# Truer durations and new places in a hand-planned two-layer Metaformer kernel, with small VectorE work moved to GpSimd

## The chip, the cores and the metric

One core of a Trainium2 chip runs the whole kernel. The metric is the device time of one execution in microseconds; the kernel before took 3854.12 us (median of three runs, 3846.69 to 3867.57). Engines are called as in the profile: PE (TensorE), DVE (VectorE), ACT (ScalarE), POOL (GpSimd) and SP (the queue that issues most transfers).

## What is computed

Two layers on an image batch `x` of (8, 256, 32, 32) in fp32, that is 8 images of 1024 tokens with 256 channels. Cut to what matters, the reference is:

```python
# layer 0
h = layernorm(x) @ W_in;  xs, z = split(h)            # 512 channels each
xs = silu(causal_conv4(xs));  dt, B, C = parts(xs @ W_x)
dt = softplus(dt @ W_dt + b_dt)
state = exp(dt * A) * state + dt * xs * B             # 16 states, over 1024 tokens
x += ((sum(state * C) + xs * Dp) * silu(z)) @ W_out
t = layernorm(x)                                      # mixture of 8 experts, best 2 per token
p = softmax(t @ gate_w + gate_b);  w = top2(p)
x += sum_e w[e] * (gelu(t @ W1[e] + b1[e]) @ W2[e] + b2[e])
# layer 1
y = layernorm(x)
x += concat(y[:128], conv3x3, conv1x11, conv11x1, mamba)   # each on 32 channels
t = layernorm(x);  r = t @ wr + br                    # of 1024 tokens the best 511
t += where(best, r * (gelu(t @ w1 + b1) @ w2 + b2), 0)
```

## The kernel before

**Tiling.** Layer 0's state-space part is cut into 16 units (8 images, two halves of 512 tokens). A unit has two channel pairs (`cp`), each of 8 steps over pairs of states, and each step handles two blocks of 128 channels by `scan_pair` (line 777): POOL multiplies dt*x with the broadcast B for two states (`dbu`, line 780, 128 x 1024), ACT makes the two exponentials (785), DVE runs two scans (788) and multiplies with C (793), and PE adds the results into the PSUM tile `y` by an identity matmul (804). In some steps POOL first adds the two products (797), which halves PE's part; the list `PAIRED` says in how many of a unit's steps. A unit has 64 scans, so 16 units have 1024; layer 1's small mamba has 32 scans for each group of two images. The scans come to 1152, and they serve below as a scale of progress. B and C rows are broadcast to all partitions by DMA (839, 1416).

**Stages.** After every unit, `tokens` projects to tokens and makes the layer norm and gate logits. After each four units (a group of 2 images, 2048 tokens) follow `route` (softmax, top 2, slots), `scatter` (the rows go to their slots by indirect DMA from POOL, `put`, 1068), `experts` (23 blocks of 256 rows: weights fetched by SP, two rounds of matmuls at 1157 and 1179, written back), `combine` (each token's two rows gathered by POOL at 1250, weighted and summed with the residual), `taps_of` (the depthwise convolutions, 26 sums on DVE, 1323), `mamba_in`, `mamba_scan`, `mamba_out`, `assemble`, `ranks` (each token's rank by counting on DVE, 1534 to 1545), `feed_forward` (best tokens to slots, two matmul layers) and `finish` (rows gathered at 1621 and added, output written).

**What sets the order.** The kernel doesn't issue its operations in the order of the text. Every stage records steps (`step`, `dma`, `gpsimd`): an engine, a duration in us, a due time, and the buffers read and written. `Flow.run` then plays the kernel through with these durations and takes, over and over, the step that can start first, with preference by due time; that gives each engine its fixed instruction order. On the chip every engine works its list strictly in order. Three kinds of numbers therefore shape the program: durations in the steps (`HOP` is the time from one engine's end to another's start, `PACE` a factor on PE's durations, `lat` the landing time of a transfer), the due times in `UNIT_AT` and `PLAN` (in units of two scans; a pair is the start and the distance of a stage's parts), and the sizes of the buffer pools (2 `ys`, 2 `wdiag`, 4 `dbu`, 4 `bc`). Where the planner sees PE idle, it puts matmuls on zeros there (`warm`, 525 and 529).

**The places concerned.** `delta` (line 747) computes softplus as max(v, 0) + ln(1 + exp(-|v|)): ACT makes |v| (754), the exponential (755) and the logarithm (756), DVE joins them into `dt` (758), and POOL multiplies dt with x (760). `small_rstd` (854) makes 1/sqrt(variance) on ACT and minus mean times that on DVE (859); `tokens` and `combine` use it. `gate` (910) turns raw logits into logits with four small DVE operations. In `combine` (1230) PE sums four products into PSUM for each block of 128 tokens:

```python
nc.tensor.matmul(at, g.ident, xc.v[:, h], start=True, stop=False)
for q in range(2):
    nc.tensor.matmul(at, ds.v[:, q], ys.v[:, q], start=False, stop=False)
nc.tensor.matmul(at, grp["cwt"].v[rows], b2[rows, blk % 4], start=False, stop=True)
```

where `ds` is a diagonal of the routing weights that ACT makes from the identity (1254), and ACT copies the sum out of PSUM (1267).

Of the kernel before, what the change touches and what calls it, by code (L numbers as in the profile page):

```python
# [38 lines left out]
N = 512  # L39
# [17 lines left out]
PAIRED = [2, 4, 0, 4, 3, 4, 7, 5, 5, 6, 8, 7, 5, 8, 6, 6, 7, 7, 5, 6]  # L57
# [5 lines left out]
    dict(put=10.59, experts=(180, 8.0), combine=(355, 4.88), taps=(436, 2.05), mamba=464, assemble=(486, 1.12), ranks=500, ffn=(521, 4.8), finish=(570, 2.4)),  # L63
    dict(put=6.24, experts=(357, 6.25), combine=(465, 1.5), taps=(550, 0.75), mamba=541, assemble=(568, 2.41), ranks=628, ffn=(722, 4.8), finish=(767, 3.75)),
    dict(put=5.3, experts=(465, 5), combine=(602, 2.94), taps=(701, 1.84), mamba=666, assemble=(681, 1.88), ranks=699, ffn=(791, 2.81), finish=(827, 2.89)),
    dict(put=2.65, experts=(603, 4), combine=(692, 0.86), taps=(761, 0.77), mamba=775, assemble=(796, 0.43), ranks=795, ffn=(836, 3), finish=(873, 3.07)),
# [30 lines left out]
HOP = 0.08  # L97
SWITCH = 1.3
PACE = 1.07
# [73 lines left out]
class Flow:  # L173
# [29 lines left out]
    def dma(self, prio, kb, run, reads=(), writes=(), fills=(), claims=(), us=0.4):  # L203
        return self.step(SP, us, prio, run, reads, writes, fills, claims, lat=2.3 + kb / 180)

    def run(self):
# [17 lines left out]
        def earliest(s):  # L224
            at = now[s.engine]
            for d in s.needs:
                at = max(at, d.end + (HOP if d.engine != s.engine or d.lat else 0.0))
# [71 lines left out]
def layers(g, ctx, x, a, out):  # L299
# [213 lines left out]
    def banks(n=1):  # L513
        return [buf("mm") for _ in range(n)]
# [232 lines left out]
    def delta(parts, dts, dtxs, xs, prio):  # L747

        v, l = banks(2), buf("sq")
        for n in range(2):  # L750
# [3 lines left out]
            step(ACT, 0.6, prio + 0.5, lambda n=n: nc.scalar.activation(l.v[:, n * N : (n + 1) * N], v[n].v, AF.Abs), [v[n]], fills=[l])  # L754
        step(ACT, 1.1, prio + 1, lambda: nc.scalar.activation(l.v, l.v, AF.Exp, scale=-1.0), [], [l], table="exp")
        step(ACT, 1.15, prio + 1, lambda: nc.scalar.activation(l.v, l.v, AF.Ln, bias=g.one), [], [l], table="exp")
        for n in range(2):
            step(DVE, 0.72, prio + 1.5, lambda n=n: nc.vector.scalar_tensor_tensor(
                dts.v[:, n], v[n].v, 0.0, l.v[:, n * N : (n + 1) * N], ALU.max, ALU.add), [v[n], l], fills=[dts])
        gpsimd(2.4, prio + 2, lambda: nc.gpsimd.tensor_tensor(dtxs.v, dts.v, xs.v, ALU.mult), [dts, xs], [dtxs])  # L760

    def dt_of(i, cp, prio):
# [6 lines left out]
        delta(parts, dts, dtxs, u[f"xs{cp}"], prio)  # L769
# [84 lines left out]
    def small_rstd(mv, rstd, shift, eps, prio, made, fill):  # L854
# [4 lines left out]
        return step(DVE, 0.6, prio, lambda: nc.vector.scalar_tensor_tensor(  # L859
            shift(), mv()[:, :, 0:1], -1.0, rstd(), ALU.mult, ALU.mult), [*made, fill[0]], fills=fill[1:])  # L860

    def tokens(i, prio):
# [47 lines left out]
        def gate():  # L910

            lg = grp["logits"].v[:, blks]
            wide = [P, nb, E]
            nc.vector.tensor_tensor(raw.v, raw.v, grp["rstd"].v[:, blks].to_broadcast(wide), ALU.mult)
            nc.vector.tensor_tensor(lg, gsum.to_broadcast(wide), grp["shift"].v[:, blks].to_broadcast(wide), ALU.mult)
            nc.vector.tensor_tensor(lg, lg, raw.v, ALU.add)
            nc.vector.tensor_tensor(lg, lg, gate_b.unsqueeze(1).to_broadcast(wide), ALU.add)

        step(DVE, 1.6, now, gate, [grp["rstd"], grp["shift"]], [raw], [grp["logits"]])

    def route(n, prio):
# [120 lines left out]
        for part in range(8):  # L1044
            step(DVE, 1.7, prio + 1 + 0.25 * part, lambda part=part: better(part), [lg], [r])
        step(DVE, 0.6, prio + 3, masks, [], [r])
        step(PE, 0.5, prio + 3, counts, [r], [pt])
        step(DVE, 1.0, prio + 3.5, sums, [pt], [r])
# [9 lines left out]
    def put(kind, dest, slots, index, src, grp, prio, name, sources):  # L1058
# [21 lines left out]
        step(POOL, 1.15, prio, run, sources, fills=[slots], lat=2.5)  # L1080
# [149 lines left out]
    def combine(n, prio, each):  # L1230
# [6 lines left out]
        for m in range(NI):  # L1237
# [600 lines left out]
```

## Time and profile before

| | us |
|---|---|
| median of the runs | 3854.12 |
| the profiled execution, its own time | 3870.05 |
| its span, first to last instruction | 3868.2 |
| scan 1025 starts | 2805.7 |
| scan 1088 ends | 2996.5 |
| no scan until | 3278.8 |
| scan 1120 ends | 3387.2 |
| no scan until | 3557.7 |
| last scan ends | 3653.1 |

The granted PE clock was 0.94 of full speed. DMA moved 676.67 MB, 175 GB/s on average. By the program's order, the first stretch without scans holds the rest of group 2's experts, group 1's assembling and ranking, and group 2's combining and taps; the second one the same stages one group later; what follows the last scan is group 3's assembling, ranking, feed-forward and finish. A group's row in the profile gives its line, engine, operation, tiles with shapes and count, then busy time and the mean of one in ns, then the idle time of the engine before it and what ended that.

```profile
DVE  4899899989679978976898898779787527557751
POOL 3567567588577768866775886545765433424522
DMA  6333333344544435535553558654669666967955
...
L780 POOL TENSOR_TENSOR dbu<-dtx,bc 128x1024 f32<-128x1024 f32 x576 | 1359.3, 2368 | 515.6 <-PE y L804 349.0
L788 DVE TENSOR_TENSOR_SCAN mm<-mm,dbu 128x512 f32<-128x512 f32 x576 | 703.9, 1222 | 229.7 <-ACT mm L785 153.8
L797 POOL TENSOR_TENSOR dbu<-dbu 128x512 f32<-128x512 f32 x370 | 480.9, 1301 | 299.4 <-DVE dbu L793 291.3
```

The digits are tenths of busy time in 40 slices of the span. VectorE is nearly full for the first three quarters and half empty in the last.

### The profile page before, as it was taken

The numbers are of one execution on the slowest core, as the hardware profiler recorded it, in microseconds if no ns is written. First come the engines' busy times: TensorE is split into PE (matmuls) and PEld (weight loads), VectorE is DVE, ScalarE is ACT, GpSimd is POOL, SyncE is SP. The second block draws the span as 40 slices with busy tenths as digits, with TensorE's granted clock in tenths as the row PEclk, the third lists the DMA queues.
The fourth block names the chain that finished last, engine by engine and source line by source line (L and its number), as shares of the span: only waits on it lengthen the run. The fifth ranks groups of instructions, "written<-read, shape, count | busy, mean of one in ns | idle before, by whom it ended". The sixth has DMA issues, their size and how long they took to land. (4 is left out here: it accounts for less than half of the span.)

```text
span 3868.2 us, 38209 instructions
## 1 busy us (share of the span) xinstructions
PE 3299.0 (85%) x10818; PEld 1849.4 (48%) x10818; DVE 2978.3 (77%) x4281; ACT 2207.2 (57%) x4010; POOL 2327.8 (60%) x1587
## 2 busy tenths in 40 slices
PE   8888888788889888978997798988987889799768
PEld 3333333333544444434553444554555666566446
DVE  4899899989679978976898898779787527557751
ACT  4555565465757557645765665665764456556433
POOL 3567567588577768866775886545765433424522
PEclk9999999999999999998999999999888989899989
DMA  6333333344544435535553558654669666967955
GB/s 232 122 123 131 114 131 132 106 151 162 200 139 167 165 129 194 181 111 172 172 174 122 195 181 226 204 184 136 200 204 223 222 213 214 243 215 215 247 175 168
DMA packets 277073, 676.67 MB, mean 175 GB/s; under 512 B 33063, under 2 KB 114349, under 8 KB 276862
## 3 DMA queue, kind: packets, MB, share of 16 engines
q1 hardware_dynamic: 258430, 623.88, 51.2%
q0 software_dynamic: 18432, 50.36, 4.1%
q8 instruction: 87, 1.43, 0.2%
q14 instruction: 124, 1.02, 0.1%
HBM read 572.92 MB, written 101.19 MB: 174 GB/s over the span
## 5 line engine op out<-in xcount | busy, mean ns | idle before, releaser
L780 POOL TENSOR_TENSOR dbu<-dtx,bc 128x1024 f32<-128x1024 f32 x576 | 1359.3, 2368 | 515.6 <-PE y L804 349.0
L804 PE MATMUL y<-dbu,ident 128*128 128x512 f32 x1564 | 822.6, 635 | 217.9 <-POOL dbu L797 185.7
L785 ACT ACTIVATE mm<-dt,neg_a 128x512 f32<-128x512 f32 x1152 | 770.3, 688 | 208.2 <-DVE dbu L793 190.4
L788 DVE TENSOR_TENSOR_SCAN mm<-mm,dbu 128x512 f32<-128x512 f32 x576 | 703.9, 1222 | 229.7 <-ACT mm L785 153.8
L793 DVE TENSOR_TENSOR dbu<-mm,bc 128x512 f32<-128x512 f32 x1152 | 796.4, 691 | 81.4 <-DMA bc<-rows 18.0
L788 DVE TENSOR_TENSOR_SCAN mm<-mm,state,dbu 128x512 f32<-128x512 f32 x576 | 738.2, 1282 | 59.5 <-POOL dbu L780 38.7
L797 POOL TENSOR_TENSOR dbu<-dbu 128x512 f32<-128x512 f32 x370 | 480.9, 1301 | 299.4 <-DVE dbu L793 291.3
L804 PEld LDWEIGHTS y<-dbu,ident 128*128 128x128 f32 x1564 | 281.6, 197 | 560.5 <-POOL dbu L797 278.7
L1179 PE MATMUL mm<-we,hid 128*128 128x256 f32 x1984 | 486.4, 398 | 36.0 <-ACT state L792 13.0
L792 ACT COPY state<-mm 128x1 f32<-128x1 f32 x576 | 91.4, 160 | 731.6 <-DVE dbu L793 710.9
L1157 PE MATMUL mm<-xbt,we 128*128 128x256 f32 x1984 | 474.3, 391 | 30.4 <-DMA we<-in_W12f 10.4
L1179 PEld LDWEIGHTS mm<-we,hid 128*128 128x128 f32 x1984 | 387.8, 199 | 156.3 <-issue 47.4
L1157 PEld LDWEIGHTS mm<-xbt,we 128*128 128x128 f32 x1984 | 383.4, 196 | 139.2 <-issue 46.9
L525 PE MATMUL y<-still 128*128 128x512 bf16 x1059 | 275.7, 395 | 0.0
L721 PE MATMUL mm<-pre,w_tap 128*128 128x512 f32 (+3 forms) x512 | 240.8, 612 | 28.6 <-ACT pre L708 27.3
L440 ACT ACT_TABLE_LOAD x176 | 225.8, 1283 | 3.1
L1250 POOL DMA_INDIRECT ys<-slots_y,slot x128 | 122.2, 954 | 160.0 <-PE mm L1262 69.0
L1163 ACT ACTIVATE hid<-mm,we 128x256 f32<-128x256 f32 x496 | 196.8, 475 | 37.8 <-PE mm L1157 29.1
L525 PEld LDWEIGHTS <-still 128*128 128x128 bf16 x1059 | 105.9, 101 | 192.6 <-issue 118.8
L721 PEld LDWEIGHTS mm<-pre,w_tap 128*128 128x128 f32 x512 | 95.5, 193 | 166.8 <-issue 103.9
L1068 POOL DMA_INDIRECT slots_x<-xg,slot x128 | 129.8, 1014 | 68.4 <-DVE acc_b L1323 31.2
L1621 POOL DMA_INDIRECT ys<-y,slot_t x64 | 63.1, 986 | 158.7 <-DVE xc L1631 59.0
(251 smaller groups left out, 3983.6 us busy)
## 6 DMA issues: line engine op xcount, KB each, us to landing
bc<-rows SPq DMA_DIRECT2D x512, 512.0 KB
bc<-rows SPq DMA_DIRECT2D x256, 256.0 KB
we<-in_W SPq DMA_DIRECT2D x92, 514.0 KB
we<-in_W SPq DMA_DIRECT2D x92, 512.0 KB
xb<-slots_x SPq DMA_DIRECT2D x92, 256.0 KB
slots_y<-xo SPq DMA_DIRECT2D x92, 256.0 KB
we<-in_W12f SPq DMA_DIRECT2D x32, 514.0 KB
xc<-x SPq DMA_DIRECT2D x64, 256.0 KB
```

What stands on the lines that cost most here:

```text
L440: nc.scalar.preload_act_table_set(tables[name])
L525: nc.tensor.matmul(live[0].v[:, 0], still, wide, start=False, stop=False)
L721: nc.tensor.matmul(tc_.v[:, cut:], w_tap[:, c, j], pre.v[:, cut + j : j + N], start=j == 3, stop=j == 0)
L780: gpsimd(2.45, prio, lambda: nc.gpsimd.tensor_tensor(dbu.v, dtxs.v[:, n : n + 1].to_broadcast(wide2), bt.v, ALU.mult), [dtxs, bt], [dbu], ...
L785: step(ACT, 0.69, prio, lambda j=j, h=h: nc.scalar.activation(h.v, dts.v[:, n], AF.Exp, scale=scales(j)), [dts], [h], table="exp", scan=True)
L788: step(DVE, 1.25, prio, lambda j=j, h=h: nc.vector.tensor_tensor_scan(h.v, h.v, dbu.v[:, j], 0.0 if initial is None else initial[1](j), AL ...
L793: step(DVE, 0.68, prio, lambda j=j, h=h: nc.vector.tensor_tensor(dbu.v[:, j], h.v, ct.v[:, j], ALU.mult), [h, ct], [dbu], scan=True)
L797: gpsimd(1.3, prio + 2.3, lambda: nc.gpsimd.tensor_tensor(dbu.v[:, 0], dbu.v[:, 0], dbu.v[:, 1], ALU.add), [], [dbu])
L804: nc.tensor.matmul(y.v[:, n], g.ident, dbu.v[:, j], start=False, stop=stop and (paired or j == 1))
L1157: nc.tensor.matmul(tv[:, f], we[0].v[:, at : at + P], xbt.v[:, k], start=k == 0, stop=k == KC - 1)
L1163: nc.scalar.activation(hid.v[:, f], tv[:, f % 2], func, bias=we[0].v[:, at : at + 1])
L1179: nc.tensor.matmul(to, hid.v[:, f, h * P : (h + 1) * P], we[1].v[:, f * C : (f + 1) * C], start=extra is None and f == 0, stop=f == FC - 1,)
```

## The change

It has four parts.

- **Durations and places.** The planner's durations of transfers (2.3 us + KB/180 becomes 3.4 us + KB/250), of indirect transfers and of several steps are set anew; a step that waits for PE now counts 0.15 us more (`DRAIN`); PE's factor goes from 1.07 to 1.05. `PLAN` and `PAIRED` get new values. None of this changes an operation, except that `PAIRED` decides where POOL adds pairs; it changes every engine's order.
- **dt.** Except in unit 0, ACT writes max(v, 0) into `dt` and POOL adds the logarithm, in place of DVE's two operations.
- **Small work.** The product in `small_rstd` becomes two POOL operations, and `gate` runs on POOL.
- **Late groups' rows.** In `combine` of groups 2 and 3 PE keeps the bias product only; DVE weights the two gathered rows onto it and adds the residual. The diagonals and ACT's copy fall away there.

The diff, with less context:

```diff
@@ -54,16 +54,16 @@
-PAIRED = [2, 4, 0, 4, 3, 4, 7, 5, 5, 6, 8, 7, 5, 8, 6, 6, 7, 7, 5, 6]
+PAIRED = [2, 2, 0, 4, 0, 5, 8, 5, 5, 7, 8, 8, 5, 5, 6, 5, 7, 7, 5, 5]
...
-    dict(put=10.59, experts=(180, 8.0), combine=(355, 4.88), taps=(436, 2.05), mamba=464, assemble=(486, 1.12), ranks=500, ffn=(521, 4.8), finish=(570, 2.4)),
-    dict(put=6.24, experts=(357, 6.25), combine=(465, 1.5), taps=(550, 0.75), mamba=541, assemble=(568, 2.41), ranks=628, ffn=(722, 4.8), finish=(767, 3.75)),
-    dict(put=5.3, experts=(465, 5), combine=(602, 2.94), taps=(701, 1.84), mamba=666, assemble=(681, 1.88), ranks=699, ffn=(791, 2.81), finish=(827, 2.89)),
-    dict(put=2.65, experts=(603, 4), combine=(692, 0.86), taps=(761, 0.77), mamba=775, assemble=(796, 0.43), ranks=795, ffn=(836, 3), finish=(873, 3.07)),
+    dict(put=2.64, experts=(180, 8.0), combine=(358, 2.93), taps=(451, 3.28), mamba=464, assemble=(496, 1.12), ranks=500, ffn=(521, 4.8), finish=(613, 2.21)),
+    dict(put=9.37, experts=(357, 6.25), combine=(505, 1.88), taps=(545, 1.2), mamba=551, assemble=(563, 2.41), ranks=630, ffn=(745, 3.84), finish=(768, 2.81)),
+    dict(put=5.28, experts=(465, 5), combine=(562, 2.94), taps=(659, 4.42), mamba=643, assemble=(684, 1.5), ranks=685, ffn=(791, 1.69), finish=(797, 4.62)),
+    dict(put=2.65, experts=(603, 4), combine=(692, 0.33), taps=(755, 1.54), mamba=775, assemble=(776, 0.43), ranks=753, ffn=(812, 3), finish=(841, 3.07)),
@@ -95,8 +95,9 @@
+DRAIN = 0.15
...
-PACE = 1.07
+PACE = 1.05
@@ -201,7 +202,7 @@
-        return self.step(SP, us, prio, run, reads, writes, fills, claims, lat=2.3 + kb / 180)
+        return self.step(SP, us, prio, run, reads, writes, fills, claims, lat=3.4 + kb / 250)
@@ -224,7 +225,7 @@
-                at = max(at, d.end + (HOP if d.engine != s.engine or d.lat else 0.0))
+                at = max(at, d.end + ((DRAIN if d.engine == PE else 0.0) + HOP if d.engine != s.engine or d.lat else 0.0))
@@ -744,7 +745,7 @@
-    def delta(parts, dts, dtxs, xs, prio):
+    def delta(parts, dts, dtxs, xs, prio, soon=False):
@@ -752,11 +753,17 @@
             step(ACT, 0.6, prio + 0.5, lambda n=n: nc.scalar.activation(l.v[:, n * N : (n + 1) * N], v[n].v, AF.Abs), [v[n]], fills=[l])
+            if not soon:
+                step(ACT, 0.6, prio + 0.6, lambda n=n: nc.scalar.activation(dts.v[:, n], v[n].v, AF.Relu), [v[n]], fills=[dts])
         step(ACT, 1.1, prio + 1, lambda: nc.scalar.activation(l.v, l.v, AF.Exp, scale=-1.0), [], [l], table="exp")
         step(ACT, 1.15, prio + 1, lambda: nc.scalar.activation(l.v, l.v, AF.Ln, bias=g.one), [], [l], table="exp")
-        for n in range(2):
-            step(DVE, 0.72, prio + 1.5, lambda n=n: nc.vector.scalar_tensor_tensor(
-                dts.v[:, n], v[n].v, 0.0, l.v[:, n * N : (n + 1) * N], ALU.max, ALU.add), [v[n], l], fills=[dts])
+        if soon:
+            for n in range(2):
+                step(DVE, 0.72, prio + 1.5, lambda n=n: nc.vector.scalar_tensor_tensor(
+                    dts.v[:, n], v[n].v, 0.0, l.v[:, n * N : (n + 1) * N], ALU.max, ALU.add), [v[n], l], fills=[dts])
+        else:
+            gpsimd(2.4, prio + 1.5, lambda: nc.gpsimd.tensor_tensor(
+                dts.v.rearrange("p n t -> p (n t)"), dts.v.rearrange("p n t -> p (n t)"), l.v, ALU.add), [l], [dts])
         gpsimd(2.4, prio + 2, lambda: nc.gpsimd.tensor_tensor(dtxs.v, dts.v, xs.v, ALU.mult), [dts, xs], [dtxs])
@@ -766,7 +773,7 @@
         ]
-        delta(parts, dts, dtxs, u[f"xs{cp}"], prio)
+        delta(parts, dts, dtxs, u[f"xs{cp}"], prio, soon=i == 0)
@@ -856,8 +863,12 @@
             nc.scalar.activation(rstd(), rstd(), AF.Exp, scale=-0.5)), made, fills=fill[:1], table="exp")
-        return step(DVE, 0.6, prio, lambda: nc.vector.scalar_tensor_tensor(
-            shift(), mv()[:, :, 0:1], -1.0, rstd(), ALU.mult, ALU.mult), [*made, fill[0]], fills=fill[1:])
+
+        def product():
+            nc.gpsimd.tensor_tensor(shift(), mv()[:, :, 0:1], rstd(), ALU.mult)
+            nc.gpsimd.tensor_scalar(shift(), shift(), -1.0, None, ALU.mult)
+
+        gpsimd(0.3, prio, product, [*made, fill[0]], fills=fill[1:])
@@ -911,12 +922,12 @@
-            nc.vector.tensor_tensor(raw.v, raw.v, grp["rstd"].v[:, blks].to_broadcast(wide), ALU.mult)
-            nc.vector.tensor_tensor(lg, lg, gate_b.unsqueeze(1).to_broadcast(wide), ALU.add)
-
...
+            nc.gpsimd.tensor_tensor(raw.v, raw.v, grp["rstd"].v[:, blks].to_broadcast(wide), ALU.mult)
...
+        gpsimd(0.8, now, gate, [grp["rstd"], grp["shift"]], [raw], [grp["logits"]])
@@ -1042,10 +1053,10 @@
-            step(DVE, 1.7, prio + 1 + 0.25 * part, lambda part=part: better(part), [lg], [r])
+            step(DVE, 1.9, prio + 1 + 0.25 * part, lambda part=part: better(part), [lg], [r])
...
-        step(DVE, 1.0, prio + 3.5, sums, [pt], [r])
+        step(DVE, 1.7, prio + 3.5, sums, [pt], [r])
@@ -1077,7 +1088,7 @@
-        step(POOL, 1.15, prio, run, sources, fills=[slots], lat=2.5)
+        step(POOL, 1.4, prio, run, sources, fills=[slots], lat=3.0)
@@ -1242,30 +1253,50 @@
             (t,), xo = banks(), buf("xo")
+
+            late = n >= 2
             for h in range(2):
                 blk = i * NI + j + h
-                ys, ds = buf("ys", line), buf("wdiag", line)
+                ys, ds = buf("ys", line), None if late else buf("wdiag", line)
                 for q in range(2):
...
                         in_offset=bass.IndirectOffsetOnAxis(ap=idx.v[:, blk : blk + 1], axis=0)),
-                        [grp["y"], idx], fills=[ys], lat=2.5)
-                    step(ACT, 0.4, now - 1, lambda q=q, ds=ds, wt=wt, blk=blk: nc.scalar.activation(
-                        ds.v[:, q], g.ident, AF.Copy, scale=wt.v[:, blk]), [wt], fills=[ds])
+                        [grp["y"], idx], fills=[ys], lat=3.3)
+                    if not late:
+                        step(ACT, 0.4, now - 1, lambda q=q, ds=ds, wt=wt, blk=blk: nc.scalar.activation(
+                            ds.v[:, q], g.ident, AF.Copy, scale=wt.v[:, blk]), [wt], fills=[ds])
...
                     at = t.v[:, h * C : (h + 1) * C]
-                    nc.tensor.matmul(at, g.ident, xc.v[:, h], start=True, stop=False)
-                    for q in range(2):
-                        nc.tensor.matmul(at, ds.v[:, q], ys.v[:, q], start=False, stop=False)
-                    nc.tensor.matmul(at, grp["cwt"].v[rows], b2[rows, blk % 4], start=False, stop=True)
-
-                step(PE, 1.9, now, product, [ys, ds, xc, grp["cwt"]], [t], claims=[xo])
+                    if ds is not None:
+                        nc.tensor.matmul(at, g.ident, xc.v[:, h], start=True, stop=False)
+                        for q in range(2):
+                            nc.tensor.matmul(at, ds.v[:, q], ys.v[:, q], start=False, stop=False)
+                    nc.tensor.matmul(at, grp["cwt"].v[rows], b2[rows, blk % 4], start=ds is None, stop=True)
+
+                def weighted(h=h, blk=blk, ys=ys, xo=xo, t=t):
+                    nc.vector.scalar_tensor_tensor(
+                        xo.v[:, h], ys.v[:, 0], grp["weight0"].v[:, blk], t.v[:, h * C : (h + 1) * C], ALU.mult, ALU.add
+                    )
+                    nc.vector.scalar_tensor_tensor(
+                        xo.v[:, h], ys.v[:, 1], grp["weight1"].v[:, blk], xo.v[:, h], ALU.mult, ALU.add
+                    )
+
+                if late:
+                    step(PE, 0.5, now, product, [grp["cwt"], xc], fills=[t], claims=[xo])
+                    step(DVE, 1.2, now + 0.2, weighted, [ys, t, grp["weight0"], grp["weight1"]], fills=[xo])
+                else:
+                    step(PE, 2.3, now, product, [ys, ds, xc, grp["cwt"]], [t], claims=[xo])
             bn = buf("bn")
-            step(ACT, 0.6, now + 0.3, lambda xo=xo, t=t: nc.scalar.copy(
-                xo.v, t.v.rearrange("p (h c) -> p h c", h=2)), [t], [xo])
+            if late:
+                step(DVE, 0.9, now + 0.3, lambda xo=xo, xc=xc: nc.vector.tensor_tensor(
+                    xo.v, xo.v, xc.v, ALU.add), [xc], [xo])
+            else:
+                step(ACT, 0.6, now + 0.3, lambda xo=xo, t=t: nc.scalar.copy(
+                    xo.v, t.v.rearrange("p (h c) -> p h c", h=2)), [t], [xo])
             dma(now + 0.5, 256, lambda xo=xo, two=two, i=i: nc.sync.dma_start(x1.v[:, two, i], xo.v), [xo], fills=[x1])
@@ -1418,7 +1449,7 @@
-                    dma(pos + 2 * sp + hf - 6, 512, fetch, [grp["rows"][hf]], [both[j]], us=0.8)
+                    dma(pos + 2 * sp + hf - 6, 800, fetch, [grp["rows"][hf]], [both[j]], us=0.9)
@@ -1486,7 +1517,7 @@
-            step(DVE, 1.9, now + 0.7, stats, [xc], [bn, junk], [tok])
+            step(DVE, 1.0, now + 0.7, stats, [xc], [bn, junk], [tok])
@@ -1621,7 +1652,7 @@
-                    [grp["y2"][i], slot], fills=[ys], lat=2.5)
+                    [grp["y2"][i], slot], fills=[ys], lat=3.3)
@@ -1638,7 +1669,7 @@
-            step(DVE, 1.3, now, added, [tok, ys], [xc])
+            step(DVE, 1.6, now, added, [tok, ys], [xc])
```

More of the change, by code (lines that the diff above doesn't have):

```diff
@@ L913, in gate @@
             wide = [P, nb, E]
-            nc.vector.tensor_tensor(raw.v, raw.v, grp["rstd"].v[:, blks].to_broadcast(wide), ALU.mult)
-            nc.vector.tensor_tensor(lg, gsum.to_broadcast(wide), grp["shift"].v[:, blks].to_broadcast(wide), ALU.mult)
-            nc.vector.tensor_tensor(lg, lg, raw.v, ALU.add)
-            nc.vector.tensor_tensor(lg, lg, gate_b.unsqueeze(1).to_broadcast(wide), ALU.add)
-        step(DVE, 1.6, now, gate, [grp["rstd"], grp["shift"]], [raw], [grp["logits"]])
+            nc.gpsimd.tensor_tensor(raw.v, raw.v, grp["rstd"].v[:, blks].to_broadcast(wide), ALU.mult)
+            nc.gpsimd.tensor_tensor(lg, gsum.to_broadcast(wide), grp["shift"].v[:, blks].to_broadcast(wide), ALU.mult)
+            nc.gpsimd.tensor_tensor(lg, lg, raw.v, ALU.add)
+            nc.gpsimd.tensor_tensor(lg, lg, gate_b.unsqueeze(1).to_broadcast(wide), ALU.add)
+        gpsimd(0.8, now, gate, [grp["rstd"], grp["shift"]], [raw], [grp["logits"]])
     def route(n, prio):
```

## The prediction

> **What bounds the kernel now.** I read the page's shares and its forty slices first, then the engines' busy time by stretch, cut where the timeline shows VectorE's scans stop or start (line 788, 1152 in all), then the groups by shape, then the waits, all and those of the first gap.
>
> ```profile
> span 3868.2 us, 38209 instructions
> PE 3299.0 (85%) x10818; PEld 1849.4 (48%) x10818; DVE 2978.3 (77%) x4281; ACT 2207.2 (57%) x4010; POOL 2327.8 (60%) x1587
> 58.00:1000.00 942.00, 807.35 (x2210) 352.09 (x2209) 860.50 (x1058) 512.56 (x910) 637.52 (x365) 0.96 0.39 133
> 1000.00:2000.00 1000.00, 865.01 (x2690) 467.82 (x2689) 818.96 (x993) 625.01 (x1104) 700.99 (x442) 0.95 0.48 162
> 2000.00:2996.50 996.50, 847.92 (x2788) 494.34 (x2787) 830.42 (x1137) 612.50 (x1102) 647.99 (x415) 0.93 0.62 187
> 2996.50:3278.80 282.30, 249.93 (x1070) 184.85 (x1070) 144.29 (x383) 147.34 (x301) 106.12 (x136) 0.94 0.67 214
> 3278.80:3387.20 108.40, 82.11 (x297) 57.04 (x296) 60.10 (x63) 60.12 (x106) 48.51 (x28) 0.87 1.01 244
> 3387.20:3557.70 170.50, 161.03 (x666) 111.96 (x665) 99.22 (x288) 96.08 (x204) 63.69 (x62) 0.96 0.67 211
> 3557.70:3653.10 95.40, 67.80 (x252) 39.40 (x251) 80.41 (x77) 54.58 (x98) 61.91 (x41) 0.93 0.96 254
> 3653.10:3868.20 215.10, 166.59 (x734) 119.45 (x732) 73.84 (x253) 75.15 (x156) 49.05 (x60) 0.89 0.56 178
> ```
>
> A row is: stretch, length, busy PE, weight loads, DVE, ACT, POOL, clock, DMA share, GB/s. Up to 2996.5 (the body, 1088 scans) DVE is busiest of the engines that do real work: 91%, then 82% and 83%. PE's 85% of the span holds 340 us of matmuls on zeros that keep its clock up (lines 525, 529). Then come two gaps without scans (282 and 170 us, PE 89% and 94%), two scan stretches whose DMA share is 1.01 and 0.96, and a tail of 215 us.
>
> ```profile
> L859 DVE SCALAR_TENSOR_TENSOR rs<-mv,rs 128x2 f32<-128x2 f32 x32 | 39.3, 1229 | 21.3 <-ACT rs L858 14.4 <-ACT rs L857 4.9 <-issue 1.2
> L859 DVE SCALAR_TENSOR_TENSOR shift<-mv,rstd 128x4 f32<-128x4 f32 x16 | 28.3, 1768 | 3.0 <-ACT rstd L858 3.0
> L758 DVE SCALAR_TENSOR_TENSOR dt<-mm,sq 128x512 f32<-128x512 f32 x72 | 46.4, 683 | 64.2 <-ACT sq L756 57.4 <-ACT state L792 6.8
> ...
> L859 DVE SCALAR_TENSOR_TENSOR rs<-mv,rs x32: 151/164/8916, 1775.7 to 3499.7; 128x2 f32<-128x2 f32 x32
> ...
> L760 POOL TENSOR_TENSOR dtx<-dt,xs 128x1024 f32<-128x1024 f32 x36 | 85.7, 2380 | 120.9 <-DVE dt L758 109.7 <-ACT xg L1579 9.3 <-ACT mm L785 1.8
> ...
> DVE mm L788 <- ACT mm L785: 174.6, 101, 9.4
> ...
> POOL slots_x L1068 <- DVE acc_b L1323: 31.2, 1, 31.2
> ```
>
> Two elements per partition take 0.16 us at the median and 8.9 at worst: DVE is held, not working. POOL stood 109.7 us for DVE's dt. The last row is gap A: POOL stood 31.2 us behind DVE, which still had group 3's routing and group 1's taps.
>
> **What the skill says.** The Trainium skill, "SBUF — State Buffer", section "Who interferes with whom": a DVE instruction with two SBUF inputs shares an exclusive port with a POOL instruction that reads SBUF, and the later one waits in full. The trace agrees: line 859 (both inputs in SBUF) has 0.164 at the median and 8.916 at most, while line 758, which reads PSUM, stays at 0.683. "GPSIMD Engine Reference", section 8, calls VectorE about twice as fast for elementwise work; here POOL's 128x512 add takes 1.301 and DVE's 0.691.
>
> **The change, part by part** (mean durations; counts from the two built programs).
>
> 1. DVE loses small_rstd's product (16 x 1.768 + 32 x 1.229 = 67.6), the gate (16 x (0.725 + 0.446 + 0.322 + 0.179) = 26.8) and dt's add but for unit 0 (68 x 0.683 = 46.4): 140.8 us, 118.4 of it in the body.
> 2. POOL gains dt's add (34 x 2.38 = 80.9), the gate (64 operations at an estimated 0.30, from 2.368 for 1024 elements and 1.301 for 512: 2.08 ns each and 0.23 fixed: 19.2) and the product as two operations (96 x 0.19, by its 3-element copy at 0.187: 18.2). PAIRED drops 22 pair additions (28.6). Net +89.7, some +84 before scan 1024, on an engine busy 65 to 70% there. Behind the add stand dt's product and the next dbu; four dbu buffers cover about two scans' pairs. In exchange the 109.7 us for DVE's dt becomes a wait for ACT alone. Cost bounds: minus 60 (half of that wait comes back as earlier dbu) to plus 84 (all on the path). I take 0 and let it reduce part 4's share.
> 3. ACT gains 68 relus (0.598: +40.7), loses 64 diagonals (0.395) and 16 copies (0.588): +6. PE loses 96 matmuls of 256 columns, two records each. Records at 0.216 (16 records in 3.45 us in the chain), so 0.432: −41, in the gaps. DVE gains 64 weightings (0.580 as line 1631) and 16 adds (0.691): +48 in the gaps; PE's wait for a gathered row becomes a wait of in-order DVE, behind which ranking stands.
> 4. Body before scan 1024 (0 to 2806): DVE −122 (part 1, and 4 taps later). The body is 14% idle and POOL gets fuller, so I take 65%: **−80**. All of it would be −122, and if POOL eats it, 0 or more.
> 5. Scans 1024 to 1088 (193 us): work comes in. Group 3's routing and scattering, 14 taps of group 1 and 70 expert matmuls (4.4 blocks of 16) make DVE 152 to 197, PE 125 to 171 (without zeros). I take **+35** (bounds 15 and 45).
> 6. Gap A (282.3): expert matmuls 332 to 198 (−58), combine's 64 to 16 (−21), transposes −6: PE −85; DVE −49 (21 taps and routing gone). It consists of 116 us until combine's first gather at 3112.3, 88 of combine, 79 to the next scan. The first loses half its expert blocks and the 31.2 us stall: 60. Combine still gathers through two ys buffers, 5 us a row block: 85. The rest has taps behind mamba's input instead of ahead: 65. Sum 210, **−72** (bounds −95, and −15 if gathers rather than matmuls set it).
> 7. The scan stretches at a DMA share of about 1 move the same bytes: **0**. A fetch planned as 800 KB is issued earlier, but the queues are full.
> 8. Gap B (170.5): expert matmuls 166 to 264 (+42), combine −21, transposes and zeros +11: PE +32; **+25** (bounds 10 and 40).
> 9. Tail: expert matmuls 230 to 196 (−15), three taps more (+5), but the chain (assemble, ranks, slots, feed-forward, gathers) has the same length: **−5** (bounds −20 and +10).
>
> SP's queue holds the same transfers in another order: group 3's scatter loads no longer stand in gap A ahead of experts' weights; I count that in part 6 only.
>
> Sum −80 + 35 − 72 + 25 − 5 = −97. The profiled execution took 3870.05 (span 3868.2, 1.9 around it), 16 above the median of the runs, 3854.12. Against the median: 3757.
>
> **Rivals.**
>
> (a) Slower: POOL takes DVE's place. Mechanism: dt's add and product hold POOL 4.75 us in a row, and each of 32 such pairs in the body lets the dbu buffers run dry. It decides once POOL is over some 85% busy where the scans run; at 800 to 1000 us it is 168 of 200 already. Price: part 4 turns from −80 into about +50 (76 for 32 adds, less a third of part 1): sum +33, **3887**. For: POOL waits 349 us for PE to free dbu, so the ring is tight. Against: those waits are slack that the additions can fill.
>
> (b) The gaps don't shrink: gathers, 5 us per block through two buffers, and DVE standing for them set gap A; part 6 is −15, sum −40, **3814**. For: POOL's 35.8 us wait for combine's matmul in gap A. Against: 85 us less on an engine at 89%.
>
> (c) More: truer durations also remove stalls of the order itself. DVE waited 174.6 us for ACT's exponentials; half gone is −87, less overlap with part 4: sum about −170, **3684**. For: many waits of 5 to 10 us where an engine's next instruction came late. Against: the reordering can make as many.
>
> That nothing changes in the order is excluded: the listing differs from the first rows on, and by whole stages in the gaps.
>
> **Numbers.** Forecast 0.45, (a) 0.20, (b) 0.17, (c) 0.18. Anything within 0.5% (about 19 us, what a measurement of this kernel can tell) counts as no change. Faster: 0.45 + 0.18 + 0.10 of (b) = 0.73. Same: 0.07 of (b) and 0.02 of (a): 0.09. Slower: 0.18. The forecast's own bounds are 3715 to 3800; the range runs from 3670, past (c), to 3885, just short of (a)'s centre, which leaves out about a tenth above and less below.
>
> **What would show it.** Right: the 1025th scan begins near 2725 instead of 2806, gap A near 210, gap B near 195, both scan stretches unchanged, POOL's wait for dt gone from VectorE. (a) shows as scans waiting for dbu more than the 110.9 us of now; (b) as gap A above 260; (c) as DVE above 90% through the body. Wrong in kind: if the scans' mean spacing before 2806 grows while DVE's work there falls.

## The result, and the profile after

The kernel after took 3825.99 us (median of 7 runs, 3818.1 to 3831.99), the kernel before beside it 3858.48 (7 runs): ratio 0.9909, 95% interval 0.9885 to 0.9934. It is faster by 0.9%; 2.5% was forecast. First the shares and two rows of slices of the kernel after, then the stretches cut at the same scans as before (stretch, length, busy PE, weight loads, DVE, ACT, POOL, clock, DMA share, GB/s).

```profile
span 3816.4 us, 38121 instructions
PE 3294.9 (86%) x10769; PEld 1846.5 (48%) x10769; DVE 2911.4 (76%) x4181; ACT 2208.1 (58%) x3999; POOL 2421.6 (63%) x1772
...
DVE  4889789879678887875899888668788757566651
...
POOL 3667478487667758987885887655774644426522
```

```profile
2787.90:3021.60 233.70, 203.67 (x737) 132.69 (x736) 196.92 (x242) 139.21 (x230) 137.93 (x101) 0.91 0.76 213
3021.60:3204.90 183.30, 160.66 (x682) 113.76 (x682) 122.43 (x326) 104.01 (x196) 83.54 (x104) 0.93 0.75 235
3204.90:3313.30 108.40, 79.55 (x289) 54.76 (x288) 65.95 (x68) 63.80 (x115) 59.50 (x39) 0.92 0.97 258
3313.30:3507.60 194.30, 184.52 (x788) 134.79 (x787) 122.18 (x325) 111.01 (x215) 75.71 (x92) 0.93 0.75 239
3507.60:3604.20 96.60, 80.06 (x279) 50.28 (x277) 71.07 (x77) 51.81 (x97) 57.31 (x35) 0.86 0.98 256
3604.20:3816.40 212.20, 154.78 (x667) 108.09 (x667) 74.30 (x252) 68.63 (x141) 50.32 (x63) 0.85 0.52 164
```

| stretch, us | before | after | change | forecast |
|---|---|---|---|---|
| to scan 1025 (the body) | 2805.7 | 2787.9 | −18 | −80 |
| scans 1025 to 1088 | 190.8 | 233.7 | +43 | +35 |
| gap A | 282.3 | 183.3 | −99 | −72 |
| scans 1089 to 1120 | 108.4 | 108.4 | 0 | 0 |
| gap B | 170.5 | 194.3 | +24 | +25 |
| scans 1121 to 1152 | 95.4 | 96.6 | +1 | 0 |
| tail | 215.1 | 212.2 | −3 | −5 |

The late stretches moved the way that was forecast, gap A a little past its bound of −95. The body didn't: the forecast's largest term brought less than a quarter. The table is of one profiled execution of each kernel. Its changes sum to −52, where the medians differ by 32, since the execution before took 3870.05 (median 3858.48) and the one after 3818.10 (median 3825.99); so some 20 us of the table belong to these two executions. The next four fences are the same two views for both kernels: first the whole body as one stretch, before and after, then what VectorE waited for in it (us in total, times, longest).

```profile
0.00:2805.70 2805.70, 2417.84 (x7277) 1235.28 (x7277) 2369.74 (x3053) 1669.78 (x2967) 1881.97 (x1194) 0.95 0.49 161
```

```profile
0.00:2787.90 2787.90, 2431.68 (x7333) 1252.08 (x7334) 2258.54 (x2895) 1669.64 (x3007) 1957.23 (x1342) 0.95 0.50 161
```

```profile
DVE mm L788 <- ACT mm L785: 164.5, 97, 9.4
DVE dt L758 <- ACT sq L756: 50.0, 7, 32.9
DVE mm L788 <- POOL dbu L780: 34.7, 15, 11.4
DVE raw L899 <- ACT xo L891: 23.1, 17, 4.0
```

```profile
DVE mm L795 <- ACT mm L792: 191.3, 114, 10.9
DVE mm L795 <- POOL dbu L787: 85.6, 37, 14.5
DVE dt L762 <- ACT sq L759: 35.9, 2, 32.9
DVE raw L910 <- ACT xo L902: 34.2, 20, 5.4
```

VectorE did lose its work: 2369.7 to 2258.5, 111 us of the 122 forecast. But its idle time in the body rose from 436.0 to 529.4, by 93. Scans (line 795 of the kernel after) wait more for their inputs, the exponentials from ACT and `dbu` from POOL. GpSimd's rows show what it took over: its waits in the body, before and then after, and three of its groups after.

```profile
POOL dtx L760 <- DVE dt L758: 103.3, 18, 14.8
```

```profile
POOL dt L765 <- ACT state L799: 28.0, 5, 11.8
POOL dt L765 <- ACT sq L759: 20.2, 7, 5.8
POOL dtx L767 <- DVE dt L762: 11.8, 1, 11.8
```

```profile
L765 POOL TENSOR_TENSOR dt<-dt,sq 128x1024 f32<-128x1024 f32 x34 | 81.9, 2409 | 92.5 <-ACT sq L759 64.5 <-ACT state L799 28.0
L869 POOL TENSOR_SCALAR rs<-rs 128x2 f32<-128x2 f32 x32 | 7.8, 242 | 2.8
L868 POOL TENSOR_TENSOR rs<-mv,rs 128x2 f32<-128x2 f32 x32 | 6.6, 208 | 19.8 <-ACT rs L865 15.6 <-DVE dbu L800 2.4 <-issue 0.8
```

The wait for VectorE's dt is gone but for unit 0 (48 us of waiting for ACT, in front of the new addition, stand in its place), and the two-element product that held VectorE 1.229 us at the mean costs GpSimd 0.45.

### The profile page after: what moved, and what is told of

Read it like the earlier page. It is cut to its first block, busy times and chain, and to the rows that moved or that the text cites. A ratio compares the mean times of both kernels' runs of the same rounds, so it can differ in the third digit from the quotient of the medians.

```text
span 3816.4 us, 38121 instructions
## 1 busy us (share of the span) xinstructions
PE 3294.9 (86%) x10769; PEld 1846.5 (48%) x10769; DVE 2911.4 (76%) x4181; ACT 2208.1 (58%) x3999; POOL 2421.6 (63%) x1772
## 5 line engine op out<-in xcount | busy, mean ns | idle before, releaser
L811 PE MATMUL y<-dbu,ident 128*128 128x512 f32 x1608 | 846.5, 636 | 214.3 <-POOL dbu L804 163.4
L804 POOL TENSOR_TENSOR dbu<-dbu 128x512 f32<-128x512 f32 x348 | 450.2, 1294 | 253.0 <-DVE dbu L800 244.4
L811 PEld LDWEIGHTS y<-dbu,ident 128*128 128x128 f32 x1608 | 292.1, 198 | 570.3 <-POOL dbu L804 256.9
L1190 PE MATMUL mm<-we,hid 128*128 128x256 f32 x1984 | 497.4, 404 | 34.0 <-ACT hid L1174 26.1
L526 PE MATMUL y<-still 128*128 128x512 bf16 x1130 | 294.8, 396 | 0.0
L1079 POOL DMA_INDIRECT slots_x<-xg,slot x128 | 128.9, 1007 | 46.4 <-ACT xg L1118 24.5
```

What stands on the lines that cost most here:

```text
L526: nc.tensor.matmul(live[0].v[:, 0], still, wide, start=False, stop=False)
L804: gpsimd(1.3, prio + 2.3, lambda: nc.gpsimd.tensor_tensor(dbu.v[:, 0], dbu.v[:, 0], dbu.v[:, 1], ALU.add), [], [dbu])
L811: nc.tensor.matmul(y.v[:, n], g.ident, dbu.v[:, j], start=False, stop=stop and (paired or j == 1))
L1190: nc.tensor.matmul(to, hid.v[:, f, h * P : (h + 1) * P], we[1].v[:, f * C : (f + 1) * C], start=extra is None and f == 0, stop=f == FC - 1,)
```

## The experiments

Theory: a microsecond taken from VectorE is worth much less than the 0.65 that part 4 counted. Rivals: GpSimd, whose added 84 us were priced at nothing, gave the gain back; the new order (durations, `DRAIN`, places, `PAIRED`) costs in the body; TensorE, at 86%, is the bound. All ratios are to the kernel before. "Order kept" means that the planner's durations stay and only the size of an operation on the chip changes, so that every engine has the same instruction list.

**What an engine's time is worth, in the same order.** Each of six kernels leaves something out. In the first pair that is dt's join in all but one column: VectorE's two operations in the kernel before, GpSimd's addition in the kernel after.

```diff
-                dts.v[:, n], v[n].v, 0.0, l.v[:, n * N : (n + 1) * N], ALU.max, ALU.add)
+                dts.v[:, n, :1], v[n].v[:, :1], 0.0, l.v[:, n * N : n * N + 1], ALU.max, ALU.add)
```

> The kernel before, every engine's order kept, but VectorE's two operations that join max(v, 0) and the logarithm into dt are cut from 512 columns to 1 (ScalarE's logarithm goes straight into dt); left out: max(v, 0) in dt, so the scans run on other values. It takes some 42 us off VectorE and gives nothing to GpSimd. Theory 1 (the body's pace is set by waits through short buffer rings and in-order engines; VectorE time that is freed becomes VectorE idle): 0 to 12 us faster than before. Theory 2 (VectorE's time was worth its full value and the work added on GpSimd ate it in the changed kernel): 30 to 45 us faster than before.

> The changed kernel, every engine's order kept, but GpSimd's addition that makes dt is cut from 1024 columns to 1 (the logarithm goes straight into dt); left out: max(v, 0) in dt. It takes some 77 us off GpSimd (34 of 2.38). Theory 1 (rings and order): at most 20 us faster than the changed kernel, so a ratio to before of 0.986 to 0.992. Theory 2 (GpSimd pays back what VectorE won): 40 to 75 us faster than the changed kernel, a ratio of 0.971 to 0.981.

Measured: 3827.51 against 3845.6, ratio 0.9949 (0.9926 to 0.9972): 20 us come back of the 38 that the two operations' busy time fell by (46.4 to 8.1), between the ranges of the two theories. Without GpSimd's addition the kernel after took 3803.7, ratio 0.9888 (0.9867 to 0.9909), only some 8 us less than with it, of 73 (81.9 to 9.0), and the two intervals overlap. GpSimd's addition isn't what ate the gain.

Larger cuts, one engine at a time: the product with C on 384 of 512 columns (VectorE), the sums of y on 384 columns (TensorE, before and after), the pair additions on 320 columns (GpSimd).

```diff
-                dbu.v[:, j], h.v, ct.v[:, j], ALU.mult), [h, ct], [dbu], scan=True)
+                dbu.v[:, j, :384], h.v[:, :384], ct.v[:, j, :384], ALU.mult), [h, ct], [dbu], scan=True)
```

> The kernel before, order kept; VectorE's multiplication with C (line 793) covers 384 of 512 columns, which leaves a quarter of the products out of the result and takes about 156 us off VectorE (128 columns at some 1.06 ns, 1152 times; 139 us of it before scan 1024). Theory 1 (rings and order set the pace, no single engine): 40 to 80 us faster, since b_dt_empty gave 20 for 42. Theory 5 (TensorE's release of dbu buffers sets it): less than 45 us. Theory of the prediction (65% and more of VectorE's time comes back): 95 us and more.

> The kernel before, order kept; TensorE's additions of the scans' products into y (line 804) cover 384 of 512 columns but for each y's last step, which leaves part of the sum out and takes about 148 us off TensorE (684 matmuls of two passes, 0.108 us each pass; some 130 us before scan 1024). Theory 5 (TensorE's release sets the pace; before's runs are about 3 us faster for each 0.001 more of granted clock): 80 to 148 us faster. Theory 1: 30 to 70 us. Theory of the prediction (VectorE bounds the body, TensorE only the gaps): less than 25 us.

> The kernel before, order kept; GpSimd's additions of pairs (line 797) cover 320 of 512 columns, which leaves part of the sum out and takes about 148 us off GpSimd (0.40 us, 370 times). GpSimd's addition stands between VectorE's product and TensorE's sum. Theory 1: 10 to 50 us faster. Theory 5: 10 to 40. If GpSimd sets the pace (rival (a)): 80 us and more. a_dt_empty, where 77 us less on GpSimd gave about 8, speaks for the low end.

> The changed kernel, order kept, with the same cut of TensorE's additions into y: about 152 us less on TensorE. Theory 5: VectorE has been relieved, so TensorE is worth at least as much as in b_pe_cut: a ratio to before of 0.955 to 0.972 where the changed kernel has 0.991. Theory 1: 0.973 to 0.983.

| cut | us removed | ratio, 95% interval | us gained |
|---|---|---|---|
| VectorE, before | 155 | 0.9775 (0.9729 to 0.9822) | 87 |
| GpSimd, before | 151 | 0.9915 (0.9890 to 0.9941) | 33 |
| TensorE, before | 138 | 1.0019 (1.0000 to 1.0039) | none |
| TensorE, after | the same cut | 0.9921 (0.9882 to 0.9961) | none beside 0.9909 |

The us removed are differences of the groups' busy times. The body as one stretch, for the cuts of VectorE, TensorE and GpSimd in the kernel before:

```profile
0.00:2719.70 2719.70, 2403.11 (x7277) 1237.43 (x7277) 2246.26 (x3053) 1667.54 (x2967) 1874.88 (x1194) 0.95 0.51 166
```

```profile
0.00:2825.60 2825.60, 2346.93 (x7278) 1253.09 (x7278) 2378.36 (x3053) 1670.10 (x2966) 1878.73 (x1194) 0.93 0.49 159
```

```profile
0.00:2768.40 2768.40, 2406.89 (x7277) 1225.90 (x7277) 2344.14 (x3053) 1669.49 (x2967) 1753.43 (x1194) 0.95 0.50 163
```

VectorE is the engine that counts, though not in full: 56% of its time came back overall. The interval of its ratio makes that 44 to 67%, so neither theory 1 nor the prediction's 65% is excluded. GpSimd's comes back at 22%, and with it VectorE's own busy time in the body fell by 26 us without any change to VectorE's work: part of what GpSimd costs seems to be VectorE held longer. (In the cut of TensorE, which leaves GpSimd's work alone, it rose by 9; the cut of GpSimd's addition in the kernel after left it as it was.)

Cutting TensorE's work brings nothing as the kernel stands. But the granted clock fell from 0.95 to 0.93 with it, and TensorE's busy time in the body fell by only 71 us. What the freed time would bring at an equal clock is open: among the 28 executions of the kernel before that stand beside this run, 0.001 less of the clock goes with about 3.3 us more, and the cut lost 0.013 on average (0.941 to 0.928), an estimated 40 us. That is a correlation and no test. The Trainium skill, "Perfetto Trace Analysis", section "Identifying the Most-Contended Engine", warns that the matmul busy share doesn't measure headroom; these runs agree: with TensorE 85% busy, a cut of its work brought nothing.

**Order and operations apart.** One kernel has the new durations, places and `PAIRED` with the operations of before; one has the new operations under the planner's numbers of before; one has the durations (with `DRAIN` and `PACE`) alone. The first is the kernel after with this (the other call of `delta` likewise), and `small_rstd` and `gate` as before:

```diff
-        delta(parts, dts, dtxs, u[f"xs{cp}"], prio, soon=i == 0)
+        delta(parts, dts, dtxs, u[f"xs{cp}"], prio, soon=True)
...
-            late = n >= 2
+            late = False
```

> The changed planner alone: new durations, PLAN and PAIRED, but dt, the small work and the late rows on the engines of before. Theory 1: the order gives nearly all of the gain (mainly the gap after scan 1088), ratio 0.988 to 0.995, since the moved operations are worth little. Theory 2: the operations' gains and losses cancel too, ratio near 0.99. If the operations carry the gain instead: 1.00.

> The moved operations alone (dt, small work, late rows), with the durations and places of before. Theory 1: between 10 us faster and 10 us slower than before, ratio 0.997 to 1.003. Theory 2: the same sum but with GpSimd's waits gone up in place of VectorE's. If moving work off VectorE is worth its 140 us wherever the stages stand: ratio 0.97.

> The new durations alone (DRAIN, PACE, transfers, steps), with the places, the PAIRED list and the operations of before. The changed planner without its operations made the stretch before scan 1024 32 us longer (2837.8 against 2805.7). Theory 3 (the durations did it: the order that they make is worse there): ratio 1.004 to 1.012 and 20 to 40 us more before scan 1024. Theory 4 (the places and PAIRED did it): ratio 0.997 to 1.003 and less than 10 us more there.

Measured: order alone 3868.38, ratio 1.0067 (1.0046 to 1.0089), its body 2837.8, 32 us longer than before; operations alone 3827.75, 0.9950 (0.9932 to 0.9969), body 2793.0; durations alone 3836.59, 0.9996 (0.9976 to 1.0017; the plain medians would give 0.997), body 2804.9. The order alone is slower, which no theory had expected. Gap A is 173.7 with the new places and no new operation, and 272.9 and 276.5 without the places: they move it. The order, taken as free in the body, costs 32 us there with the operations of before; from it the operations bring 50 (2837.8 to 2787.9). On the other path the operations bring only 13 (2805.7 to 2793.0), and the order then 5 more. The two effects don't add: +0.7% and −0.5% alone, −0.9% together. Which piece of the order costs the 32?

Three kernels take one piece out of the kernel after: `PAIRED` as before; `DRAIN = 0.0`; and no matmuls on zeros (`WARM = False`, which also frees TensorE).

> The changed kernel with the PAIRED list of before, so 22 more additions of pairs on GpSimd and 22 fewer matmuls of 512 columns on TensorE. Theory 4 in the form that dropping pairs keeps dbu buffers on TensorE longer: 10 to 25 us faster than the changed kernel before scan 1024, a ratio to before of 0.984 to 0.988. If PAIRED doesn't matter: 0.989 to 0.993.

> The changed kernel with DRAIN at 0, so the planner no longer counts 0.15 us from TensorE's end to the next engine. Theory 3 with DRAIN as the part that matters: at least 15 us faster than the changed kernel before scan 1024, ratio to before 0.984 to 0.988. If only the order's luck matters: within 10 us either way, 0.988 to 0.994. If DRAIN does what it is for: slower than the changed kernel, 0.993 or more.

> The changed kernel without the 1373 matmuls on zeros, nothing else: the order of all other work stays. If these matmuls stand where TensorE isn't idle on the chip, they delay the release of dbu buffers (GpSimd waits 344.6 us for that before scan 1024): 20 to 60 us faster. If they are hidden and hold the clock up (granted 0.935): slower, 20 us or more, with a lower clock or longer matmuls.

Measured: with `PAIRED` as before 0.9950 (0.9934 to 0.9967), body 2803.0; with `DRAIN` 0 0.9903 (0.9878 to 0.9928), body 2774.9; without the zeros 0.9946 (0.9933 to 0.9959), body 2805.7. The old `PAIRED` is slower by 0.4%, against both expectations. `DRAIN` makes no difference that can be told. Without the zeros TensorE's clock over the span was 0.884 instead of 0.935, and the kernel was a little slower; the freed TensorE time and the lower clock act together there.

**What a new order does by itself.** No piece explained the 32 us, so the next run changes nothing but how the planner breaks near-ties, in both kernels; a third puts the places of before into the kernel after.

```diff
-HOP = 0.08
+HOP = 0.10
```

> The kernel before with one number of the planner's cost model changed by 0.02 us (HOP 0.08 to 0.10). Not an operation, a stage or a price changes; the greedy planner merely breaks its near-ties in another way, so that thousands of instructions stand elsewhere. It measures how far a new order alone moves the time. If the 32 us that the new places cost before scan 1025 are such noise of the order, this run moves that stretch by 10 to 30 us in either direction (2775 to 2835 instead of 2806) and the ratio lies anywhere within 0.993 to 1.007. If an order made anew is worth next to nothing (the 32 us then are a systematic cost of the new stage places), the stretch stays within 6 us of 2806 and the ratio within 0.9985 to 1.0015.

> The same change of 0.02 us on the kernel after. Noise of the order: the stretch before scan 1025 lies between 2758 and 2818 instead of 2788, and the ratio to the kernel before between 0.984 and 0.998 (0.991 for the kernel after). No noise: 2782 to 2794 and 0.9895 to 0.9925.

> The kernel after with the PLAN (the places of the stages) of the kernel before; its operations, durations, DRAIN, PACE and PAIRED stay. If the places cost the 32 us before scan 1025 and bring the 99 of the first gap: 0 to 1024 near 2760, scans 1025 to 1088 near 175, the first gap near 275, gap B near 170, sum about 3812, ratio 0.991 or so (the gain and the cost of the places cancel in part). If the durations cost the 32: 0 to 1024 stays near 2790, and the sum is near 3850, ratio 1.0. Noise of the order: anything between.

The kernel before under the new order took 3898.52: ratio 1.0102 (1.0068 to 1.0135), slower by about as much as the whole change gained, and outside both ranges expected. Its body as one stretch, and what VectorE waited for there:

```profile
0.00:2850.70 2850.70, 2459.66 (x7459) 1254.02 (x7459) 2368.59 (x3055) 1664.83 (x2962) 1889.07 (x1200) 0.95 0.48 158
```

```profile
DVE mm L788 <- ACT mm L785: 152.3, 97, 7.6
DVE mm L788 <- POOL dbu L780: 70.7, 22, 11.5
DVE dt L758 <- ACT sq L756: 65.0, 13, 32.9
DVE raw L899 <- ACT xo L891: 37.1, 22, 3.2
```

VectorE's busy time is that of before within 1.2 us, GpSimd's and ACT's within about 7; the 45 us are idle time of VectorE, spread over many short waits like the one for `dbu`. No work was added but zeros: the planner, which puts them where it sees TensorE idle, now puts 1449 such matmuls instead of 1274, and TensorE's busy time in the body rose by 42 us (2417.8 to 2459.7). That these cost the 45 isn't excluded, but taking all zeros out of the kernel after brought nothing. The kernel after with the same 0.02 us went the other way: 0.9882 (0.9853 to 0.9912), body 2768.1. With the places of before it took 3839.16, 0.9952 (0.9936 to 0.9967), body 2816.6, so the body is longer with the old places under the new operations and longer with the new places under the old operations: neither sign belongs to the places. The profiled executions that leave nothing out, one of each kernel, split at scan 1025 (another `PAIRED` also moves 22 additions between GpSimd and TensorE):

| operations | order | body | the rest |
|---|---|---|---|
| before | before | 2805.7 | 1062.5 |
| before | new durations | 2804.9 | 1023.2 |
| before | HOP 0.10 | 2850.7 | 1034.1 |
| before | after | 2837.8 | 1040.6 |
| after | before | 2793.0 | 1037.2 |
| after | after, places of before | 2816.6 | 1014.5 |
| after | after, PAIRED of before | 2803.0 | 1026.0 |
| after | after, DRAIN 0 | 2774.9 | 1035.6 |
| after | after, HOP 0.10 | 2768.1 | 1041.8 |
| after | after | 2787.9 | 1028.5 |

The means are 2824.8 and 2790.6 for the body, 1040.1 and 1030.6 for the rest. The operations are then worth −34 us in the body (standard error about 14, from the scatter of 4 and 6 orders, which are no random draw) and about −10 in the rest; within one set of operations the order moves the body by up to 48. What share of the 32 us belongs to one number of the new planner stays open; a cost of this size needs no cause of its own.

**A version beside both.** If GpSimd has a price and TensorE none, pair additions should go back to TensorE: each entry of `PAIRED` is halved, 156 additions instead of 348, and repeated under two other orders whose unhalved kernels had been timed.

```diff
-PAIRED = [2, 2, 0, 4, 0, 5, 8, 5, 5, 7, 8, 8, 5, 5, 6, 5, 7, 7, 5, 5]
+PAIRED = [1, 1, 0, 2, 0, 2, 4, 2, 2, 3, 4, 4, 2, 2, 3, 2, 3, 3, 2, 2]
```

> The kernel after with each entry of PAIRED halved: 156 pair additions on GpSimd instead of 348 (192 x 1.294 = 248 us less), and 192 more matmuls of y sums on TensorE (about 83 us more). The theory that GpSimd's time is worth 10 to 22% and TensorE's nothing: 25 to 55 us faster than the kernel after, ratio 0.977 to 0.985, a version that beats both. The rival, that TensorE has no slack to take them (it is 86% busy, and in the cut of 148 us its clock fell instead): the 83 us come back at half or more, ratio 0.99 to 1.005.

> The kernel after with PAIRED halved (192 fewer pair additions on GpSimd, 192 more matmuls on TensorE) and HOP 0.10 in the planner: the halving under the second of three orders. Since a change of 0.02 in HOP alone moved the kernel before by 1.0% and the kernel after by -0.3%, one run of the halving is no proof. If it is worth its 25 to 55 us by itself, this kernel is faster than the kernel after with HOP 0.10 (ratio 0.9882) by 0.5% or more: 0.975 to 0.984. If the first halved run was a lucky order, the ratio lies between 0.984 and 0.998.

> The same halving with DRAIN 0: the third order, to be set beside the kernel after with DRAIN 0 (ratio 0.9903). Worth by itself: 0.977 to 0.985. A lucky order in the first: 0.985 to 1.0.

| order | unhalved | halved, 95% interval | median us halved |
|---|---|---|---|
| after | 0.9909 | 0.9834 (0.9809 to 0.9858) | 3793.41 |
| HOP 0.10 | 0.9882 | 0.9871 (0.9855 to 0.9887) | 3798.51 |
| DRAIN 0 | 0.9903 | 0.9837 (0.9817 to 0.9858) | 3787.52 |

All three are faster than their partners, by 0.5% on average: 20 us of 248 on GpSimd, less than the 25 to 55 expected, and in the second order the gain is inside the interval and the ratio in the range of a lucky first order. The body isn't where it comes from (halved 2777.9 on average, unhalved 2777.0); scans 1025 to 1088 lost 11 us and the rest 9. So it isn't shown that GpSimd's price is what came back: in the first of them GpSimd's busy time in the body fell from 1957 to 1752 us and the body by 9. A rival is TensorE's clock, which was 0.948 to 0.949 on average over the executions of the halved kernels and 0.935 to 0.939 over those of their partners; no run holds it fixed. Two of the three are 0.7% below the kernel after and beat both kernels, part of it perhaps by the order.

## Why the prediction was wrong

**Part 4, the body, failed.** It read "−122 of DVE's work, I take 65%: −80", and put GpSimd's added work and the new order at 0; −18 was measured. The zero for the order, which no reason was given for, is the step that failed most clearly.
- The order. The prediction allowed for stalls that go (rival c) or are made ("the reordering can make as many"), but put no size on it for the forecast. A nudge of the order moved the body by 45 us. With the operations of before the new planner moved it by +32, with those of after by −5. The kernel before also happened to have one of the two shortest bodies of its four orders. The −18 of the table is therefore −50 of the operations and +32 of the order on one path, and −13 and −5 on the other; how much of the missing 62 us is the order's stays open.
- GpSimd's added 84 us (75 in the trace). "I take 0" was wrong in kind: at the 11 to 22% measured they cost 8 to 17 us.
- The share. Over the whole kernel, in an unchanged order, VectorE's time was worth 51% (dt's join; interval 28 to 74%) and 56% (product with C; 44 to 67%). Both lie below 65%, and neither interval excludes it. Of the work, 111 of the 122 us came as busy time. Counted one by one, the operations that left took 133 us in the body, more than the 118.4 of part 1, because the products that are held stand there; others grew. With half of the 111, and GpSimd's price, the operations come to an estimated −39 to −48, beside −50 and −13 on the two paths and −34 ± 14 over all orders.

One operation that grew is the depthwise sum of 128 x 1024, the same 64 in both kernels, from 1622 to 1789 ns at the mean; before, then after:

```profile
L1323 DVE SCALAR_TENSOR_TENSOR acc_a<-pad_a,taps_a,acc_a 128x1024 f32<-128x1024 f32 x64 | 103.8, 1622 | 1.2
```

```profile
L1354 DVE SCALAR_TENSOR_TENSOR acc_a<-pad_a,taps_a,acc_a 128x1024 f32<-128x1024 f32 x64 | 114.5, 1789 | 1.3
```

The median is 1285 ns in both. The sums above 1400 ns are 11 before and 19 after, and each of these ran while GpSimd had a two-input operation running (so did 12 of the 45 short ones after), which fits the shared port of the Trainium skill, "SBUF — State Buffer", section "Who interferes with whom", that the prediction named. It isn't simply that GpSimd is fuller: the mean is 1795 in the kernel before with only VectorE's product cut, and 1804 in the kernel after without GpSimd's addition. Which operations meet depends on the times, and no run here isolates it.

**Parts 5 to 9 held, with a reservation.** The stretches moved by +43, −99, 0, +24, +1 and −3 against +35, −72, 0, +25, 0 and −5. Gap A was the furthest off: combine's gathers started 58 us into the gap (60 by the parts), took 68 to the last weighting instead of 85, and the next scan began 57 later instead of 65; 4 us a row block, not 5. The counting of which stage's work falls into which stretch was sound. But it mostly moves work to and fro: summed over these stretches the change is −34, and the 0.02 us in `HOP` alone brought −28 there with gap A at 277.6. The 1062.5 us of the kernel before are also the longest rest in the table above, and the four cuts in its own order, with somewhat less work, have 1021 to 1054; part of the −34 is probably that one execution.

**Rivals.** (a), slower through GpSimd, fell: scans did wait for `dbu` more (110.9 to 143.1 us over the span), as its sign said, but cutting 73 us of the suspected addition gave back 8. Its price of +50 doesn't follow from its terms either: 76 less a third of part 1's 118.4 is 37. (b) came nearest in size (3814) but by another way, since its mechanism, a gap A that doesn't shrink, didn't happen. (c), fewer stalls, came out with the opposite sign: VectorE's wait for the exponentials in the body rose from 164.5 to 191.3.

The signs listed: the 1025th scan near 2725 was missed by 63; gap A and gap B were met within 27 and 1, the scan stretches within 2; GpSimd's wait for VectorE's dt went.

## What to carry to other kernels

Where several in-order engines are 60 to 90% busy and a planner interleaves them, price work by what a cut of that engine returns in an unchanged order (here about 0.5 for VectorE, 0.1 to 0.2 for GpSimd, and nothing for TensorE, whose clock fell with the cut), and give the engine that takes the work over a price too. Before reading a change of about 1% as the work of an edit, remake the order with a meaningless nudge: if that moves the time as far, compare means over several orders, before and after.

## What the runs showed of the hardware

- With TensorE 85% busy, a cut of 138 us of its real work changed the time by +0.2% (0.0 to +0.4%) and the granted clock of the body from 0.95 to 0.93. What it would have brought at an equal clock isn't shown.
- Without the matmuls on zeros the kernel after's TensorE clock over the span fell from 0.935 to 0.884, and the time rose from 0.9909 to 0.9946 of before: keeping the clock up that way bought about 0.4%, no more than an order can, with TensorE's freed time set against it.
- Cutting 151 us from GpSimd's additions took 26 us off VectorE's busy time in the body, with VectorE's work unchanged.
- Of the kernel after's 64 depthwise sums on VectorE (median 1.285 us), 19 took over 1.4 us, the longest 7.184; all 19 ran while GpSimd had a two-input operation running.
